# Four more source tiles of the dense products of layer 3 run beside the max-pooling layer, and early products are handed out by the load of TensorE

## The chip, the core and the metric

The kernel runs on one core of a Trainium2 chip. The time is the device time of one launch in microseconds (us). Five engines work side by side, each through its own instructions in order: TensorE (PE in the profile; PEld is its loading of weights), VectorE (DVE), ScalarE (ACT), GpSimd (POOL) and SyncE (SP). SP, ACT and POOL also issue transfers between the main memory and the buffers on the chip.

## The reference

A graph network on 6250 nodes and 100000 edges that are sorted by their target. `x` has 256 features, the hidden layers 512.

```python
def _sage_mean(h, src, dst, n, deg, W_self, W_neigh, b):
    msum = segment_sum(h[src], dst, num_segments=n)
    return h @ W_self + (msum / clip(deg, 1.0)[:, None]) @ W_neigh + b
def _sage_pool(h, src, dst, n, deg, W_pool, b_pool, W_self, W_neigh, b):
    hp = relu(h @ W_pool + b_pool)
    hmax = segment_max(hp[src], dst, num_segments=n)
    hmax = where(deg[:, None] > 0, hmax, 0.0)
    return h @ W_self + hmax @ W_neigh + b
def _sage_gcn(h, src, dst, n, deg, W_neigh, b):
    msum = segment_sum(h[src], dst, num_segments=n)
    return ((msum + h) / (deg + 1.0)[:, None]) @ W_neigh + b

h = maximum(layernorm(x), 0.0)
h = _sage_mean(h, ...)      # layer 1
h = _sage_pool(h, ...)      # layer 2, max-pooling
h = _sage_gcn(h, ...)       # layer 3
h = _sage_mean(h, ...)      # layer 4
return x + h @ W_fc + b_fc
```

## The kernel before

**Tiles.** The nodes are cut into 49 node tiles of 128 (`NT`), the edges into 782 edge tiles of 128 (`T`). For an edge tile, POOL gathers the rows of the 128 source nodes from a table in main memory by an indirect transfer, one instruction for each tile. Where a node tile has very many edges (12 node tiles in layer 1, the first 23 in layers 3 and 4, `H3` = 23) the sum is computed another way: a dense table of counts, how many edges lead from each node of a source tile to each node of the node tile, is multiplied with the rows of the source tile on TensorE. So layer 3 has 254 gathers for node tiles 23 to 48, and dense products for 23 node tiles x 49 source tiles. One dense product is a pair of matmuls, one with the high and one with the low part of the rows (L637 and L632). Its counts are loaded as 8-bit numbers (`ae` early, `ac` late) and widened by ACT (`aw`, `af`).

**Layer 2** goes through all 782 edge tiles in six blocks, in the order 100, 130, 180, 220, 100 and 52 tiles. Per edge tile (counted by `at`): POOL gathers the rows `X` (L1870), DVE takes one step of a running maximum (L1843), and SP stores the stepped rows for every two tiles (L1849). At the end of a block the maximum is carried on (`carry`): TensorE transposes the last rows (`ptcf`, L1536), DVE scans along them (L1548), TensorE turns the result back (`pcf`, L1576), and SP stores a mended row (L1582). Beside this `done2(d)` finishes the node tiles 48 to 0 one after the other: it gathers the maxima (`tot`, L1678), transposes them (L1710), multiplies with the weights (L1717, L1720, L1723), splits the result in a high and a low part (L1730 to L1739) and stores them in the table `tab_r` that layer 3 gathers from (L1746, L1747). When a node tile is begun follows the list `PACE`.

**Early products.** The result of a node tile is at once a source tile of layer 3. For source tiles 10 to 41 (`EARLY`) the dense products are taken while layer 2 still runs: four source tiles make a batch, and a batch has 23 units, one for each node tile. A unit is: SP loads its counts (`ae`, 64 KB, L1802, six units ahead, 14 buffers), ACT widens them (`aw`, L1789), ACT lays the sum so far into the accumulator (`pd<-acc`, L1782), TensorE does four pairs (L632, L637), and ACT takes the sum out (`acc<-pd`, L1774). In all these are 736 pairs. They are handed out by `early.advance(...)` after each edge tile, in an even line from `at` = 320 to 752.

**Layer 3** (`sums`) issues the 254 gathers into a ring of 10 row buffers (L549); for each one DVE makes a one-hot matrix (`hot`, L545) and TensorE multiplies the two (L571, L574). Between them a `Hub` hands out its list of other work evenly over 228 of the gathers: the products of the source tiles that were not early, in four chunks for each node tile, (0, 4), (4, 10), (42, 45) and (45, 49), 23 x 17 = 391 pairs; then `turn_to_4` (L2039), which loads rows `own` and starts the stream of counts for layer 4; then 46 products of layer 4. The counts `ac` come by ACT's queue (L1970), four chunks ahead, and each load is issued when a buffer comes free; ACT widens the chunk after the next (L1979). `done3` (L2049) finishes a node tile on DVE.

So the order of each engine's work is fixed in the program; what is free is when each one gets there.

Of the kernel before, what the change touches and what calls it, by code (L numbers as in the profile page):

```python
# [34 lines left out]
UP3 = float(2 ** 12)  # L35
ROOM3, SEEN3 = float(2 ** 28), float(2 ** 11)
EARLY = (10, 42)
MADE_AT = 64
EARLY_AT = 310
SLOTS = (10, 14)  # L40
PACE = ((112, 0), (318, 19), (612, 37), (746, 49))
# [49 lines left out]
def fast_path(  # L91
# [18 lines left out]
    FH = W1_self.shape[1]  # L110
    FO = W_fc.shape[1]
    NT = (N + P - 1) // P
# [3 lines left out]
    T = (E + P - 1) // P  # L116
# [11 lines left out]
    for d in range(NT):  # L128
        m, s = _edges_below(d * P, E, N)
        m1, s1 = _edges_below((d + 1) * P, E, N)  # L130
# [9 lines left out]
    for d in range(NT):  # L140
        m, s = _edges_below(d * P, E, N)
        m1, s1 = _edges_below((d + 1) * P, E, N)
# [7 lines left out]
    H1, H3, H4 = HUB  # L150
# [105 lines left out]
    at = 0  # L256
# [390 lines left out]
    ahead = upto2.enter_context(tc.tile_pool(name="ahead", bufs=1, side="right"))  # L647
# [805 lines left out]
    with tc.tile_pool(name="fl2c", bufs=1) as ck, ExitStack() as late:  # L1453
# [244 lines left out]
        def done2(d):  # L1698
            tots, th = totals(d)
            apart = EARLY_AT < at < T - 72  # L1700
            for _ in range(6):
                yield
            hm = tots[0]
            for t in tots[1:]:
                nc.vector.tensor_tensor(hm, hm, t, op=ALU.max)
            yield
            yield from apart_by(3 if apart else 0)
            pt = bank(pst, "pt", "pt_hTf", (KH, P))
            for j in range(KH):
                nc.tensor.transpose(pt[:, j, :], hm[:, j * P : (j + 1) * P], ident)  # L1710
            yield
            hT = wk.tile([P, KH, P], F32, name="hTf")
            nc.scalar.copy(hT, pt)  # L1713
            yield
            pm = bank(psb if EARLY_AT < at < T - 40 else psd, "pb", "pm_prf")
            for k in range(KI):
                nc.tensor.matmul(pm, th[:, k, :], usA[:, k, :], start=(k == 0), stop=False)  # L1717
            yield
            for k in range(KI):
                nc.tensor.matmul(pm, th[:, KI + k, :], usB[:, k, :], start=False, stop=False)  # L1720
            yield
            for c in range(KH):
                nc.tensor.matmul(pm, hT[:, c, :], un[:, c, :], start=False, stop=(c == KH - 1))  # L1723
                if c == 1:
                    yield
            yield
            yield
            yield
            hi, lo = r2 = row_parts(d)
            nc.scalar.copy(hi, pm)  # L1730
            yield
            yield from apart_by(2 if apart else 0)
            while d == last_begun and not last_turn:
                yield
            with behind(last_turn):
                nc.tensor.matmul(pm, minus_r, hi, start=False, stop=True, skip_group_check=True)
            yield
            yield from apart_by(2 if apart else 0)
            nc.scalar.copy(lo, pm)  # L1739
            look_at(d, hi, hT)  # L1740
            if EARLY[0] <= d < EARLY[1]:
                ready.append((d, r2))
                if len(ready) == BATCH or d == EARLY[0]:
                    early_products()
            yield from apart_by(8 if apart else 0)
            nc.sync.dma_start(tab_r[d * P : (d + 1) * P, :FH], hi.bitcast(F32))  # L1746
            nc.sync.dma_start(tab_r[d * P : (d + 1) * P, FH:], lo.bitcast(F32))  # L1747
            yield
# [9 lines left out]
                    held_by[d] = last[i]  # L1758
                last[i] = d
        assert all(d >= EARLY[0] for d in held_by.values())  # L1760
        early_all = H3 * (EARLY[1] - EARLY[0])
        ready = []
        early = Hub(look=6)
        early_pool, split_pool = [], []
# [26 lines left out]
        def early_products():  # L1791
            batch = dict(ready)
            ss = sorted(batch)
            ready.clear()
            over.update({s: len(early.work) + H3 * len(ss) for s in ss})
            for d in range(H3):
                got = {}
                loaded.append(got)

# [52 lines left out]
        def paced(at):  # L1852
            for (a0, n0), (a1, n1) in zip(PACE, PACE[1:]):
                if at < a1:
                    break
            return n0 + (n1 - n0) * (at - a0) / (a1 - a0)

        tiles, begun2, begun_at = [], 0, 0
        ends = []
        now = []  # L1860
        at = 0
        for b in reversed(range(NB)):
# [3 lines left out]
            for s0 in range(0, tb, G2):  # L1866
                X = (xmore if at // G2 % 2 else xpool).tile([P, G2, FH], F32, name="X2")
                for k in range(G2):
# [44 lines left out]
                    if copies and not hub.left():  # L1913
                        copies.pop(0)()
                    if at > EARLY_AT + 10:
                        early.advance(math.ceil(early_all * (at - EARLY_AT - 10)
                                                / (T - 40 - EARLY_AT)))
                    if b == 0 and s0 == 0 and k == 0:
                        for _ in finding:
                            pass  # L1920
# [83 lines left out]
    with ExitStack() as on:  # L2004
# [44 lines left out]
        with tc.tile_pool(name="fl3", bufs=2) as wk:  # L2049
# [36 lines left out]
                nc.sync.dma_start(xq[d * P : (d + 1) * P, :], q[:, :FO])  # L2086
                yield 1

            late = ((0, 4), (4, KEPT), (EARLY[1], 45), (45, NT))
            Z3 = {s: tuple(v[:, slot[s], :] for v in kept_rows) for s in range(KEPT)}  # L2090
            with tc.issue_after(kept_stores[-1].ins):
                for s0, s1 in ((EARLY[1], NT),):
                    Z3.update(resident(zw, tab_r, FH, s0, s1))
            block = stream(zw, [(d, s0, s1) for d in range(H3) for s0, s1 in late], zw, ahead=1)
            todo = []
            work = []
            for d in range(H3):
                work += dense([s for s0, s1 in late for s in range(s0, s1)], lambda s, d=d: block(d, s), lambda s: Z3[s], FH, psd,
                              lambda acc, d=d: todo.append(done3(d, acc)), own=d)
            work += [turn_to_4] + turns[0][1]  # L2100
            sums(wk, psg, tab_r, FH, srcE, keyE, jb, H3, done3, 10, Hub(work), wait=14, todo=todo,
# [683 lines left out]
```

## Time and profile before

| | us |
|---|---|
| median of three runs | 2477.61 |
| lowest and highest of them | 2477.28, 2480.75 |
| the profiled execution, its own time | 2482.45 |
| its span, first to last instruction | 2480.6 |
| layer 2 with early products, in the trace | 1116 to 1760 |
| layer 3, in the trace | 1784 to 2146 |

The share of the span in which each engine is busy is 86% for TensorE, 77% for DVE, 58% for ACT and 70% for POOL; the mean granted clock of TensorE is 0.939 of full speed. These are averages over stages with different limits, so the rows further down are taken from the two stages of the change. In such rows a time in brackets, or behind the second bar, is how long the engine stood idle just before, and the arrow names what ended that idle time. Issuing of transfers by SP and ACT isn't counted as busy.

### The profile page before, as it was taken

What the parts mean: (1) busy time and instruction counts of PE and PEld (TensorE: products, weight loads), DVE (VectorE), ACT (ScalarE), POOL (GpSimd) and SP (SyncE); (2) the same over time, 40 slices, a digit from 0 to 9 for tenths busy, and PEclk for the clock granted to TensorE, in tenths of its full rate; (3) what the DMA queues carried; (4) which work ended last, traced back from release to release, by engine and by line L of the source; (5) the groups of instructions that cost most, each with busy time, mean ns of one, the idle gap of its engine ahead of it and who ended that gap; (6) DMA issues with size and microseconds to landing.
All of it is one profiled execution on the core that took longest, in us unless ns stands there. A gap on an engine that the chain in (4) does not pass through costs nothing.

```text
span 2480.6 us, 35381 instructions
## 1 busy us (share of the span) xinstructions
PE 2143.6 (86%) x9402; PEld 1239.8 (50%) x9402; DVE 1915.2 (77%) x5404; ACT 1430.8 (58%) x2891; POOL 1739.2 (70%) x2013
## 2 busy tenths in 40 slices
PE   4689999999688477479979995999799998799997
PEld 2356666676444233134434442455344444477776
DVE  7899987785789898978868788786567776477655
ACT  5898878676378898855545663655222222244443
POOL 5477776677566776777767777777477777477776
PEclk9799999999899688689989997999899999999999
DMA  9677777777999999999999999999899999899997
GB/s 314 197 232 240 223 209 213 218 221 242 294 334 317 329 366 349 332 349 363 361 312 358 356 361 365 321 360 348 296 378 405 407 407 407 310 351 335 335 305 237
DMA packets 381103, 784.91 MB, mean 316 GB/s; under 512 B 59374, under 2 KB 175830, under 8 KB 380860
## 3 DMA queue, kind: packets, MB, share of 16 engines
q0 software_dynamic: 135184, 471.64, 56.6%
q1 hardware_dynamic: 178984, 252.38, 28.2%
q10 hardware_dynamic: 66724, 58.54, 7.3%
q8 instruction: 76, 1.25, 0.2%
q14 instruction: 135, 1.11, 0.1%
HBM read 573.21 MB, written 209.94 MB: 316 GB/s over the span
## 4 chain that ended last, share of the span: by engine, by line
PE 37%; DMA 35%; DVE 15%; issue 5%; POOL 4%; ACT 3%; ACTq 0%; POOLq 0%; DVEq 0%; SPq 0%
DMA X<-rows,srcIf 13%; PE pd L632 6%; PE pd L637 6%; PE pd L629 4%; DVE run L1843 4%; DMA rows<-X 3%; DMA xq<-acc 3%; DMA ring<-tab_s,srcE 3%; PE pm_w L292 3%; POOL X L1870 3%; DVE X L1843 3%; PE pm_hp L1278 3%; PE pg L571 2%; PE pg L574 2%; PE pm_hp L1272 2%
## 5 line engine op out<-in xcount | busy, mean ns | idle before, releaser
L1870 POOL DMA_INDIRECT X<-rows,srcIf x782 | 746.5, 955 | 302.5 <-issue 151.5
L1843 DVE SCALAR_TENSOR_TENSOR run<-run,samef,X 128x512 f32<-128x512 f32 x758 | 572.6, 755 | 76.5 <-DMA X<-rows,srcIf 70.7
L549 POOL DMA_INDIRECT ring<-tab_h,srcT x402 | 389.8, 970 | 174.9 <-issue 40.5
L1979 ACT CAST af<-ac 128x768 fp32r<-128x768 fp8e4 (+3 forms) x299 | 217.5, 735 | 352.9 <-PE pd L629 122.4
L549 POOL DMA_INDIRECT ring<-tab_r,srcE x254 | 258.4, 1017 | 99.1 <-issue 39.4
L1843 DVE SCALAR_TENSOR_TENSOR X<-X,samef,run 128x512 f32<-128x512 f32 x379 | 282.2, 745 | 54.7 <-DMA X<-rows,srcIf 22.8
L549 POOL DMA_INDIRECT ring<-tab_s,srcE x254 | 245.3, 966 | 94.8 <-PE pg L569 25.3
L603 DVE SCALAR_TENSOR_TENSOR acc<-pg,M,acc 128x256 f32<-128x256 f32 (+2 forms) x556 | 281.3, 532 | 31.5 <-PE pg L574 21.3
L574 PE MATMUL pg<-ring,hot 128*128 128x256 f32 (+1 forms) x656 | 293.3, 455 | 0.0
L637 PE MATMUL pd<-kept_rows,aw 128*128 128x512 f32 x552 | 277.0, 584 | 0.0
L571 PE MATMUL pg<-ring,hot 128*128 128x259 f16 (+1 forms) x656 | 212.0, 326 | 35.5 <-DMA ring<-tab_h,srcT 14.5
L632 PE MATMUL pd<-kept_rows,ae 128*128 128x512 f16 x552 | 215.0, 390 | 7.0 <-DMA ae<-tab_a 5.3
L1774 ACT COPY acc<-pd 128x512 f32<-128x512 f32 x184 | 107.8, 586 | 181.8 <-PE pd L637 181.5
L637 PE MATMUL pd<-Z1h,af 128*128 128x256 f32 x588 | 194.8, 364 | 0.4 <-ACT af L1306 0.4
L1723 PE MATMUL pm_prf<-unf,hTf 128*128 128x512 f32 x384 | 188.6, 615 | 1.1 <-ACT hTf L1713 1.1
L458 PE MATMUL pb<-hm,hs 128*128 128x196 bf16 x480 | 102.2, 271 | 92.3 <-DVE hm L442 60.2
L545 DVE TENSOR_SCALAR hot<-iota_bf,keyE 128x128 fp32r<-128x128 bf16 x508 | 137.7, 297 | 54.8 <-PE pg L574 28.1
L629 PE MATMUL pd<-zt,af 128*128 128x512 f32 x598 | 165.5, 396 | 2.4 <-ACT af L1979 2.4
L632 PEld LDWEIGHTS <-ae 128*128 128x128 fp8e4 x736 | 71.0, 96 | 186.4 <-issue 171.3
L632 PE MATMUL pd<-Z1l,A 128*128 128x259 f16 x588 | 158.5, 280 | 0.0
L574 PEld LDWEIGHTS pg<-ring,hot 128*128 128x128 f32 x656 | 130.8, 199 | 53.7 <-issue 45.2
L464 ACT ACTIVATE A<-pb 128x392 fp8e4<-128x392 f32 x240 | 116.8, 497 | 60.6 <-PE pb L458 59.7
(439 smaller groups left out, 5122.3 us busy)
## 6 DMA issues: line engine op xcount, KB each, us to landing
rows<-X SPq DMA_DIRECT2D x385, 256.0 KB
rows<-hpf SPq DMA_DIRECT2D x49, 256.0 KB
X<-rows,srcIf POOLq DMA_INDIRECT x782
th<-tab_t SPq DMA_DIRECT2D x48, 256.0 KB
ae<-tab_a SPq DMA_DIRECT2D x184, 64.0 KB
tab_a<-A ACTq DMA_DIRECT2D x15, 784.0 KB
ac<-tab_a ACTq DMA_DIRECT2D x115, 96.0 KB
tab_t<-th SPq DMA_DIRECT2D x37, 256.0 KB
```

The lines of the kernel that those rows point to most:

```text
L545: nc.vector.tensor_scalar(hot[j], iota_b, keyT[:, j - jb : j - jb + 1], None, op0=ALU.is_equal)
L549: nc.gpsimd.indirect_dma_start(out=ring[:, j % deep, :].bitcast(F32), out_offset=None, in_=table, in_offset=bass.IndirectOffsetOnAxis(ap=s ...
L571: nc.tensor.matmul(pg[:, : F + counts], hot[j].bitcast(BF16)[:, 1::2], X.bitcast(F16)[:, 2 * F : 3 * F + counts], start=(k == 0), stop=False)
L574: mm = nc.tensor.matmul(pg[:, :F], hot[j], X[:, :F], start=False, stop=(k == n - 1))
L603: nc.vector.scalar_tensor_tensor(acc[d], half, m, acc[d], op0=ALU.mult, op1=ALU.add)
L629: nc.tensor.matmul(hold[0], a[0], z, start=(s == ss[0]), stop=(s == ss[-1]))
L632: nc.tensor.matmul(hold[0][:, : F + extra], a[1], z[1][:, : F + extra], start=(s == ss[0] and hold[1]), stop=False, **more)
L637: nc.tensor.matmul(hold[0][:, :F], a[0], z[0], start=False, stop=(s == ss[-1]), **more)
L1723: nc.tensor.matmul(pm, hT[:, c, :], un[:, c, :], start=False, stop=(c == KH - 1))
L1843: stepped[:] = [nc.vector.scalar_tensor_tensor(put, held, st, row, op0=ALU.mult, op1=ALU.max)]
L1870: nc.gpsimd.indirect_dma_start(out=X[:, k, :], out_offset=None, in_=tab_p, in_offset=bass.IndirectOffsetOnAxis(ap=srcI[:, t : t + 1], axis=0),
L1979: nc.scalar.copy(wide[i][:, :n, :], got[i][:, :n, :])
```

## The change

A ninth early batch takes source tiles 6 to 9, for node tiles 0 to 11 only (`EARLY_KEPT`). It adds 12 units with 48 pairs to the early products (784 in place of 736) and takes them out of layer 3 (343 in place of 391), where the chunk (4, 10) becomes (4, 6) for these 12 node tiles. The rate at which early pairs are handed out is no longer even: `early_to` counts each node tile that is begun by `PACE` as 17 pairs (`TILE_PAIRS`) and keeps the sum of both even.

```diff
+EARLY_KEPT = (6, 12)
+TILE_PAIRS = 17
...
-            if EARLY[0] <= d < EARLY[1]:
+            if EARLY_KEPT[0] <= d < EARLY[1]:
                 ready.append((d, r2))
-                if len(ready) == BATCH or d == EARLY[0]:
+                if len(ready) == BATCH or d == EARLY_KEPT[0]:
                     early_products()
...
-        early_all = H3 * (EARLY[1] - EARLY[0])
+        early_all = H3 * (EARLY[1] - EARLY[0]) + EARLY_KEPT[1] * (EARLY[0] - EARLY_KEPT[0])
...
-            over.update({s: len(early.work) + H3 * len(ss) for s in ss})
-            for d in range(H3):
+            h = H3 if ss[0] >= EARLY[0] else EARLY_KEPT[1]
+            over.update({s: len(early.work) + h * len(ss) for s in ss})
+            for d in range(h):
...
+        def early_to(at):
+            a0, a1 = EARLY_AT + 10, T - 32
+            n0 = paced(a0)
+            load = early_all + TILE_PAIRS * (NT - n0)
+            return math.ceil(load * min(1.0, (at - a0) / (a1 - a0)) - TILE_PAIRS * (paced(min(at, PACE[-1][0])) - n0))
...
-                        early.advance(math.ceil(early_all * (at - EARLY_AT - 10)
-                                                / (T - 40 - EARLY_AT)))
+                        early.advance(early_to(at))
...
-            late = ((0, 4), (4, KEPT), (EARLY[1], 45), (45, NT))
+            late = [((0, 4), (4, EARLY_KEPT[0] if d < EARLY_KEPT[1] else KEPT), (EARLY[1], 45),
+                     (45, NT)) for d in range(H3)]
...
-            block = stream(zw, [(d, s0, s1) for d in range(H3) for s0, s1 in late], zw, ahead=1)
+            block = stream(zw, [(d, s0, s1) for d in range(H3) for s0, s1 in late[d]], zw, ahead=1)
...
-                work += dense([s for s0, s1 in late for s in range(s0, s1)], lambda s, d=d: block(d, s), lambda s: Z3[s], FH, psd,
+                work += dense([s for s0, s1 in late[d] for s in range(s0, s1)], lambda s, d=d: block(d, s), lambda s: Z3[s], FH, psd,
```

In the changed program the lines of the early products and of layer 2 stand two to nine further down (L632 is L634, L637 is L639, L1536 is L1538, L1802 is L1805, L1849 is L1852, L571 is L573).

TensorE's program around the transposes `ptcf` at the end of the block of 220 edge tiles, before; the rows L632 and L637 are early pairs, L1720 and L1723 belong to `done2`:

```order
L1720 MATMUL pm_prf_18142<-usB_10239,th2_17821 128x512 x2
L632 LDWEIGHTS ae_17989
L632 MATMUL pd_18127<-kept_rows1_11381,ae_17989 128x512
L637 MATMUL pd_18127<-kept_rows0_11380,aw_18098 128x512
L632 LDWEIGHTS ae_17989
L632 MATMUL pd_18127<-kept_rows1_11381,ae_17989 128x512
L1536 MATMUL ptcf_18380<-identf_97,X2_18359 128x128 x4
L637 MATMUL pd_18127<-kept_rows0_11380,aw_18098 128x512
L1723 MATMUL pm_prf_18142<-unf_10240,hTf_18131 128x512 x2
```

The same place after:

```order
L639 MATMUL pd_18373<-r2h_13_18102,aw_18349 128x512
L634 LDWEIGHTS ae_18235
L634 MATMUL pd_18373<-r2l_12_17893,ae_18235 128x512
L639 MATMUL pd_18373<-r2h_12_17892,aw_18349 128x512
L1712 MATMUL pt_hTf_18404<-identf_97,tot_18282 128x128
L1538 MATMUL ptcf_18658<-identf_97,X2_18640 128x128 x4
L1712 MATMUL pt_hTf_18404<-identf_97,tot_18282 128x128 x3
```

Before, these transposes follow 495 early pairs, of a batch whose rows are in `kept_rows`; after, they follow 562, of the batch with source tiles 10 to 13 (`r2h_13`, `r2l_12`).

SyncE's queue around the store of the mended row of that block (L1582, `fixf`), before; `rows2<-X2` are the stepped rows, `ae` the counts of early pairs:

```order
L1849 DMA rows2_72<-X2_18529 128x512
L1802 DMA ae_18551<-tab_a_70 128x256
L1849 DMA rows2_72<-X2_18548 128x512
L1802 DMA ae_18573<-tab_a_70 128x256
L1849 DMA rows2_72<-X2_18570 128x512
L1802 DMA ae_18597<-tab_a_70 128x256
L1582 DMA rows2_72<-fixf_18506 128x512
L1802 DMA ae_18623<-tab_a_70 128x256
```

After:

```order
L1852 DMA rows2_72<-X2_18771 128x512
L1805 DMA ae_18627<-tab_a_70 128x256
L1852 DMA rows2_72<-X2_18791 128x512
L1693 DMA th2_18969<-tab_t_67 128x512
L1852 DMA rows2_72<-X2_18813 128x512
L1805 DMA ae_18650<-tab_a_70 128x256
L1852 DMA rows2_72<-X2_18829 128x512
L1584 DMA rows2_72<-fixf_18769 128x512
L1748 DMA tab_r_68<-kept_rows0_11380 128x512
```

Behind the block's end fewer loads of counts stand between the stores of rows, and a load for `done2` and a store of a finished node tile have come in.

TensorE's program in layer 3 about the 91st gather, before; `pg` is the sum over gathered rows, `pd` a dense sum:

```order
L571 MATMUL pg_21262<-ring_20161,hot_21224 128x512
L574 MATMUL pg_21262<-ring_20161,hot_21224 128x512
L632 LDWEIGHTS ac_21168
L632 MATMUL pd_21207<-zt42_20149,ac_21168 128x512
L637 MATMUL pd_21207<-zt42_20149,af_21245 128x512
L632 LDWEIGHTS ac_21183
L632 MATMUL pd_21207<-zt42_20149,ac_21183 128x512
L637 MATMUL pd_21207<-zt42_20149,af_21286 128x512
L571 LDWEIGHTS hot_21239
```

After:

```order
L573 MATMUL pg_21447<-ring_20349,hot_21407 128x512
L576 MATMUL pg_21447<-ring_20349,hot_21407 128x512
L639 MATMUL pd_21477<-kept_rows0_11380,af_21478 128x512
L634 LDWEIGHTS ac_21393
L634 MATMUL pd_21477<-kept_rows1_11381,ac_21393 128x512
L639 MATMUL pd_21477<-kept_rows0_11380,af_21478 128x512
L573 LDWEIGHTS hot_21426
```

Where two pairs of dense products stood between two gathers, there are now fewer than two on average, and each node tile's list is in another place.

## Rows read from the trace of the kernel before

**Rows 1.** By stretches: window, length, busy PE, PEld, DVE, ACT, POOL, clock, DMA, GB/s
```profile
1116.00:1545.00 429.00, 385.49 (x1423) 187.07 (x1422) 349.98 (x558) 231.07 (x452) 316.50 (x334) 0.95 1.00 354
1545.00:1760.00 215.00, 207.71 (x763) 102.18 (x761) 165.09 (x249) 119.35 (x234) 157.11 (x165) 0.98 0.99 341
...
1845.00:2085.00 240.00, 236.09 (x1011) 106.94 (x1010) 180.28 (x409) 62.74 (x114) 184.65 (x179) 0.99 1.03 407
```

**Rows 2.** Timeline of POOL in layer 2: start, duration, instruction, [idle before <-releaser]
```profile
1399.27 0.95 POOL L1870 DMA_INDIRECT X<-rows,srcIf  x1 [0.30 <-issue]
1400.52 0.95 POOL L1870 DMA_INDIRECT X<-rows,srcIf  x1 [0.30 <-DVE X L1843]
```

**Rows 3.** POOL's groups, 1116 to 1760 us: count, busy, mean ns, idle before
```profile
L1870 POOL DMA_INDIRECT X<-rows,srcIf x463 | 441.1, 953 | 157.1 <-issue 96.0 <-DVE X L1843 20.4 <-DVE run L1843 20.1
```

**Rows 4.** POOL's groups, 1784 to 2104 us
```profile
L549 POOL DMA_INDIRECT ring<-tab_r,srcE x241 | 245.6, 1019 | 88.1 <-issue 37.5 <-PE pg L574 16.6 <-DVE oddI L79 13.9
```

**Rows 5.** Timeline of POOL in layer 3
```profile
1953.87 0.95 POOL L549 DMA_INDIRECT ring<-tab_r,srcE  x1 [0.30 <-PE pd L637]
...
1956.37 1.36 POOL L549 DMA_INDIRECT ring<-tab_r,srcE  x1 [0.30 <-issue]
...
1960.80 1.50 POOL L549 DMA_INDIRECT ring<-tab_r,srcE  x1 [0.30 <-DMA ring<-tab_r,srcE]
```

**Rows 6.** Timeline of TensorE in layer 3
```profile
1950.60 0.39 PE L571 MATMUL pg<-ring,hot 128*128 128x512 f16 x1
...
1951.06 0.39 PE L632 MATMUL pd<-kept_rows,ac 128*128 128x512 f16 x1
...
1951.52 0.39 PE L632 MATMUL pd<-kept_rows,ac 128*128 128x512 f16 x1
```

**Rows 7.** Timeline of TensorE at the end of the block of 220
```profile
1516.45 0.39 PE L632 MATMUL pd<-kept_rows,ae 128*128 128x512 f16 x1
1544.65 1.09 PE L1536 MATMUL ptcf<-identf,X 128*128 128x128 f32 x4 [27.81 <-DVE X L1843]
```

**Rows 8.** SyncE's waits, 1116 to 1790 us: line <- released by: us, times, longest
```profile
SPq L1802 <- PE pd L632: 19.0, 18, 3.6
SPq L1802 <- PE pd L637: 16.7, 22, 1.9
```

**Rows 9.** ScalarE's groups by form, 1116 to 1784 us
```profile
L1789 ACT CAST aw<-ae 128x512 fp32r<-128x512 fp8e4 x183 | 113.7, 622 | 16.4 <-DMA ae<-tab_a 16.3
L1774 ACT COPY acc<-pd 128x512 f32<-128x512 f32 x184 | 107.8, 586 | 181.8 <-PE pd L637 181.5
```

**Rows 10.** POOL's groups at the end of layer 3, 2104 to 2146 us
```profile
L549 POOL DMA_INDIRECT ring<-tab_r,srcE x13 | 12.8, 984 | 11.0 <-PE pg L574 8.5 <-issue 1.9 <-PE pd L629 0.3
```

**Rows 11.** Timeline of POOL there
```profile
2110.86 1.05 POOL L549 DMA_INDIRECT ring<-tab_r,srcE  x1 [3.01 <-PE pg L574]
...
2119.94 0.95 POOL L549 DMA_INDIRECT ring<-tab_r,srcE  x1 [3.21 <-PE pg L574]
```

**Rows 12.** Timelines of TensorE, ScalarE and SyncE there
```profile
2109.55 0.61 PE L571 MATMUL pg<-ring,hot 128*128 128x512 f16 x1 [5.34 <-DVE hot L545]
...
2107.78 0.40 ACT L332 CAST q<-acc 128x256 fp32r<-128x256 f32 x1 [13.12 <-DMA own<-tab_r]
...
2085.77 6.04 SPq L2045 DMA_DIRECT2D own<-tab_r  x5
```

**Rows 13.** Timeline of ScalarE in layer 3: loads of counts (ACTq) and their casts
```profile
1896.92 0.33 ACTq L1970 DMA_DIRECT2D ac<-tab_a  x1
...
1903.65 0.51 ACT L1979 CAST af<-ac 128x384 fp32r<-128x384 fp8e4 x1 [1.56 <-DMA ac<-tab_a]
...
1905.49 0.33 ACTq L1970 DMA_DIRECT2D ac<-tab_a  x1
...
1913.40 0.84 ACT L1979 CAST af<-ac 128x768 fp32r<-128x768 fp8e4 x1 [2.95 <-DMA ac<-tab_a]
```

**Rows 14.** All waits, 1783 to 2120 us
```profile
PE pd L637 <- ACT af L1979: 2.0, 2, 1.7
```

## The prediction

> **What bounds the kernel now.** I read the view by stretches first, then the POOL groups of the two stages that the change touches, then the timelines of POOL and TensorE inside them, and last the views of waits. The two stages are layer 2, from where the early products begin (1116 us) to its last gather (1760 us), and layer 3 (1784 to 2146 us).
>
> By stretches [rows 1], TensorE looks like the bound of both: 385.5 of 429 us and 207.7 of 215 us busy in layer 2, and 236.1 of 240 us in the middle of layer 3. POOL shows only 316.5 of 429 and 184.7 of 240 us. The reader is to distrust both numbers: between two gathers POOL has idle time that is the same every time. In layer 2 a gather is busy 0.95 us after 0.30 us idle, whether the row puts the idle to issue or to DVE [rows 2]. So 1.25 us is the least from one gather to the next. From 1116 to 1760 us there are 334 + 165 = 499 POOL operations [rows 1], nearly all of them gathers of 0.953 us [rows 3]; 499 x 1.25 = 624 of 644 us. POOL is issuing for 97% of the stretch, and all waits together cost at most 20 us. In layer 3, 241 gathers of 1.019 us [rows 4] at 0.30 us between make 241 x 1.32 = 318 of the 320 us from 1784 to 2104. The gap is 0.30 us there too, whether the releaser is a product (PE pd L637) or issue [rows 5]. Had TensorE held POOL up, these gaps would be longer than the plain ones. POOL's issue bounds both stages; TensorE has just kept step.
>
> The Trainium skill ("Perfetto Trace Analysis", Identifying the Most-Contended Engine) would have GpSimd judged by its occupancy, and says that the busy share of matmuls is a poor measure for TensorE. By the first half POOL has 23% of room in layer 3 and is not the bound, which would leave rival A; the constant gap of 0.30 us [rows 2, 5] speaks against that reading, and the trace agrees with the second half. The sum below goes by the gap.
>
> **The change part by part.** It moves 48 pairs of products (12 node tiles x 4 source tiles) from layer 3 to layer 2, with 12 loads of 64 KB. It also hands out all 784 early pairs by a new rule: 1.96 pairs per edge tile up to the 612th, then 1.48, where before it was 736/432 = 1.70 throughout. (Worked out: 784 pairs plus 17 for each of the 29.9 node tiles still to begin are 1292 over 430 edge tiles, 3.00 each; of these, tiles begun take 17 x 18/294 = 1.04 up to the 612th and 17 x 12/134 = 1.52 after.)
>
> *TensorE in layer 3.* From one product or gather's pair to the next is 0.46 us [rows 6]. The 48 pairs are 48 x 0.46 = 22 us. Before, 391 + 47 = 438 items are spread over 254 - 14 - 12 = 228 gathers, 1.92 each, so a gather costs TensorE 2.92 x 0.46 = 1.34 us; after, 390 items, 1.71 each, 2.71 x 0.46 = 1.25 us. POOL takes 1.32 us for it. TensorE goes from level with POOL to a little below it. Since POOL sees no wait beyond 0.30 us, I take 0 for this; the ends are -22 us (TensorE bound it after all) and +3 us (the work after the products now falls three gathers earlier).
>
> *TensorE in layer 2.* The 22 us come in here, and most pairs earlier. The cover is a wait: at the end of the block of 220 edge tiles TensorE comes at 1516.8 us to the transposes L1536 and stands 27.8 us until DVE's last running maximum [rows 7]. In program order 495 early pairs stand before these transposes, and 562 after the change: 67 x 0.46 = 31 us more, so TensorE comes there at about 1548, 3 us late instead of 28 us early. So the wait is filled. Behind it 736 - 495 = 241 pairs remained, now 222, 9 us less, in the stretch that was fullest (207.7 of 215 us). I take 0 for TensorE itself: the last gather is POOL's.
>
> *SyncE.* SyncE's stores of the stepped rows free the buffers that POOL gathers into. Its loads of counts stand in the same queue, and waited for products 19.0 + 16.7 = 36 us [rows 8]. A load waits where TensorE is late with the product that frees its buffer, and TensorE is latest just behind the wait of 27.8 us. With that wait filled, less is late there. Only part of it reached POOL, whose whole loss is 20 us. I take -2 us, between -10 and +7 (the second end is rival C).
>
> *ScalarE.* 12 more widenings of 0.622 us and 24 copies of 0.586 us [rows 9], 21.5 us, beside 231 us of work in 429 us [rows 1]: hidden, 0. If they had no cover they would delay products, not gathers. In layer 3, 12 casts become shorter.
>
> *Transfers.* 12 x 64 KB = 0.79 MB go from layer 3, where 407 GB/s moved at a busy share of 1.03, to layer 2 at 354 GB/s [rows 1]: -1.9 us and +2.2 us if transfers bound both stages. In layer 3 POOL's gathers take 1.019 us against 0.953 us; some are 1.2 to 1.5 us [rows 5], which fits full queues, and 241 x 0.066 = 16 us is the most that a lighter load could return. The load falls by 0.6%, so I take -1.5 us there and +1 us in layer 2.
>
> *The end of layer 3.* POOL waits 11.0 us over 13 gathers for TensorE, less 13 x 0.30 = 3.9, which is 7.1 us too much, most of it at two places [rows 10, 11]. The reason isn't TensorE's load: at 2109.55 it stood 5.3 us for the one-hot matrix from DVE. DVE was held by ScalarE, whose cast stood behind the loads of layer 4's counts and waited 13.1 us, put down to the rows own<-tab_r, whose loads SyncE began at 2085.8 us [rows 12]. The step that issues these loads comes after 343 of 390 items and not after 391 of 438, three gathers earlier; everything in its shadow moves with it. I take 0, between -7 and +3 us.
>
> Sum: 0 + 0 - 2 + 0 - 1.5 + 1 + 0 = -2.5 us. On the profiled execution, 2482.45 us with a span of 2480.6 us, that is 2480. This execution lies 4.8 us above the median of the three runs, 2477.61, so against that median I say **2475 us**, with its own range from 2469.5 to 2480.5.
>
> **The rivals.**
>
> A. *TensorE bounds layer 3.* For it: 236.1 of 240 us busy, and its 1.34 us per gather is no less than POOL's 1.32. Against it: the gap that never grows. Then 228 x (1.34 - 1.25) = 20 us and the 2.5 us above go: 2455 us.
>
> A2. *The end of layer 3 loosens.* With fewer products TensorE has caught up before the two waits [rows 11], and the ring of ten gathered rows absorbs them: -7.1 - 2.5 gives 2468 us. Against it: the releaser behind the first is a transfer's landing [rows 12].
>
> B. *Slower: the look-ahead of layer 3's counts becomes too short.* The loads run four chunks ahead, each when a buffer comes free, and a cast comes 6.7 and 7.9 us after its load [rows 13]; the cast waits for the landing. Four chunks were 17 products, 17/1.92 x 1.33 = 11.8 us. For the 12 node tiles they are 13, 13/1.71 x 1.33 = 10.1 us. The cast itself takes 0.5 to 0.8 us [rows 13], so some 0.9 us must be left: from a delay of 9.2 us on TensorE waits, and POOL behind it through the ring. At 10.5 us that is 12 x 1.3 = 16 us, less what the ring holds, say 5: +11, 2489 us. Against it: 7.9 is below 9.2, and that stage had only 2.0 us of products waiting for a cast [rows 14].
>
> C. *Slower: layer 2's queue fills.* TensorE comes to the block's end with 31 us more of work in front of it and, without the wait, has no idle time left to catch up with. Loads of counts then find their 14 buffers in use earlier and SyncE's waits double, another 36 us. POOL lost at most 20 us beside the first 36; at a fifth this is +7, 2485 us. It decides if TensorE comes to L1536 later than some 1560 us, 15 us after DVE is done.
>
> D. *It does nothing*: the gains are taken up by other waits, 2477 us.
>
> **How the numbers follow.** About 0.2% (5 us) is what a measurement of this kernel can tell from no change. Forecast 0.50, of which 0.14 is faster by more than 5 us and 0.36 within; A 0.16 and A2 0.11, faster; D 0.06, same; B 0.08 and C 0.09, slower. Faster 0.14 + 0.16 + 0.11 = 0.41, same 0.36 + 0.06 = 0.42, slower 0.17. Both signs outside the forecast have weight, so the range takes in A2 and C whole, and leaves out most of A (0.14) and of B (0.06): 2460 to 2486.
>
> **What the profile after would show.** Right: the wait before L1538 (L1536 before) of the block of 220 falls from 27.8 us to under 4; SyncE's waits for products fall well below 36 us; layer 3's gathers still start 1.32 us apart with TensorE's busy share there down by about 7 points; layer 3 has the same length within 3 us. Wrong: if layer 3 from its first to its last gather is over 10 us shorter, TensorE bound it (A); if products there wait for casts over 10 us, B; if SyncE's waits for products grow and POOL's gaps with them, C. The forecast falls if either stage changes its length by more than 8 us.

## The result

The changed kernel is a little slower: 2487.72 us (median of 20 runs) against 2481.45 us (20 runs of the kernel before beside them), a ratio of 1.0028 (95% interval 1.0017 to 1.0039). In a second comparison it was 1.0020 (1.0005 to 1.0035). The forecast was 2475 us in a range to 2486. A part of the miss is the base: the median of three runs that it went out from, 2477.61, is 3.8 us below that of twenty. The rest of the miss, 8.9 us, is the gain of 2.5 us that didn't come and a cost of 6.3 us in its place.

The profiled execution after took 2496.45 us, at the upper end of its runs, so a single difference between the two profiles says little; below, stages are compared over several profiles. By stretches of the changed kernel (columns as in [rows 1]; the first three windows answer to the three there):

```profile
1118.00:1547.00 429.00, 407.15 (x1510) 197.20 (x1509) 344.70 (x548) 249.85 (x485) 309.56 (x328) 0.97 1.00 347
1556.00:1771.00 215.00, 203.16 (x739) 98.95 (x738) 164.93 (x249) 114.01 (x223) 154.47 (x163) 0.97 0.98 343
1856.00:2096.00 240.00, 224.80 (x931) 104.08 (x930) 177.20 (x403) 60.65 (x115) 174.91 (x176) 0.99 1.02 398
```

TensorE's busy time moved as the working said: 407 us where it had 385, 203 where it had 208, and 225 of 240 us in layer 3 where it had 236. POOL issued 328 operations in 429 us where it had issued 334, and 176 in 240 us where it had issued 179. So TensorE's load was moved as planned, and the engine that sets the pace became slower in both stages.

TensorE at the end of the block of 220 edge tiles, after:

```profile
1556.49 0.60 PE L1538 MATMUL ptcf<-identf,X 128*128 128x128 f32 x4
1568.18 0.66 PE L1578 MATMUL pcf<-identf,cTf 128*128 128x128 f32 x2 [9.85 <-DVE cTf L1554]
```

The wait of 27.8 us [rows 7] is gone: the row L1538 has no bracket. A wait of 9.85 us for DVE's scan comes in behind it. SyncE's waits for products fell from 36 to 27 us [rows 8]:

```profile
SPq L1805 <- PE pd L639: 16.6, 22, 1.7
SPq L1805 <- PE pd L634: 10.2, 15, 2.4
```

But POOL's group of layer 2 (1119 to 1770 us) has longer idle times put down to DVE (32.7 and 18.4 us, where there were 20.1 and 20.4 [rows 3]); busy time, mean ns and idle time stand behind the bars:

```profile
L1879 POOL DMA_INDIRECT X<-rows,srcIf x461 | 437.2, 948 | 170.7 <-issue 95.0 <-DVE run L1846 32.7 <-DVE X L1846 18.4
```

At the end of layer 3 (timeline of POOL, after), the two waits of [rows 11] are still there, the first one earlier and longer, and the wait for layer 4's first gather, 17.66 us before, is 13.38 us:

```profile
2121.59 0.95 POOL L551 DMA_INDIRECT ring<-tab_r,srcE  x1 [6.42 <-PE pg L576]
...
2138.19 1.20 POOL L551 DMA_INDIRECT ring<-tab_r,srcE  x1 [3.26 <-PE pg L576]
2159.05 0.96 POOL L551 DMA_INDIRECT ring<-tab_s,srcE  x1 [13.38 <-DMA ac<-tab_a]
```

### The profile page after: what moved, and what is told of

Read it like the earlier page. It is cut to its first block, busy times and chain, and to the rows that moved or that the text cites. A ratio compares the mean times of both kernels' runs of the same rounds, so it can differ in the third digit from the quotient of the medians.

```text
span 2494.7 us, 35434 instructions
## 1 busy us (share of the span) xinstructions
PE 2163.9 (87%) x9402; PEld 1253.8 (50%) x9402; DVE 1915.7 (77%) x5404; ACT 1444.8 (58%) x2927; POOL 1726.1 (69%) x2013
## 4 chain that ended last, share of the span: by engine, by line
PE 40%; DMA 32%; DVE 16%; issue 5%; ACT 4%; POOL 3%; SPq 0%; ACTq 0%; DVEq 0%; POOLq 0%
DMA X<-rows,srcIf 12%; PE pd L639 6%; PE pd L634 6%; PE pd L631 5%; DMA xq<-acc 5%; DVE run L1846 4%; DMA rows<-X 3%; PE pm_hp L1280 3%; PE pm_w L294 3%; DVE X L1846 3%; POOL X L1879 2%; PE pm_hp L1274 2%; PE pg L573 2%; DMA ring<-tab_s,srcE 2%; PE pg L576 2%
## 5 line engine op out<-in xcount | busy, mean ns | idle before, releaser
L1987 ACT CAST af<-ac 128x640 fp32r<-128x640 fp8e4 (+4 forms) x299 | 211.3, 717 | 353.8 <-PE pd L631 125.6
L551 POOL DMA_INDIRECT ring<-tab_r,srcE x254 | 251.2, 989 | 113.9 <-PE pg L576 37.2
L639 PE MATMUL pd<-kept_rows,aw 128*128 128x512 f32 x600 | 300.4, 585 | 0.0
L634 PE MATMUL pd<-kept_rows,ae 128*128 128x512 f16 x600 | 235.0, 392 | 12.3 <-ACT pd L1784 6.7
L573 PE MATMUL pg<-ring,hot 128*128 128x259 f16 (+1 forms) x656 | 211.5, 325 | 37.3 <-DMA ring<-tab_r,srcE 22.6
L1776 ACT COPY acc<-pd 128x512 f32<-128x512 f32 x196 | 115.0, 586 | 203.0 <-PE pd L639 202.7
L639 PE MATMUL pd<-Z1h,af 128*128 128x256 f32 x588 | 194.8, 364 | 1.0 <-ACT af L1308 1.0
L634 PEld LDWEIGHTS <-ae 128*128 128x128 fp8e4 x784 | 75.9, 97 | 201.2 <-issue 187.5
L634 PE MATMUL pd<-Z1l,A 128*128 128x259 f16 x588 | 158.5, 280 | 0.0
```

Of the source, the lines that this page charges most:

```text
L551: nc.gpsimd.indirect_dma_start(out=ring[:, j % deep, :].bitcast(F32), out_offset=None, in_=table, in_offset=bass.IndirectOffsetOnAxis(ap=s ...
L573: nc.tensor.matmul(pg[:, : F + counts], hot[j].bitcast(BF16)[:, 1::2], X.bitcast(F16)[:, 2 * F : 3 * F + counts], start=(k == 0), stop=False)
L634: nc.tensor.matmul(hold[0][:, : F + extra], a[1], z[1][:, : F + extra], start=(s == ss[0] and hold[1]), stop=False, **more)
L639: nc.tensor.matmul(hold[0][:, :F], a[0], z[0], start=False, stop=(s == ss[-1]), **more)
L1987: nc.scalar.copy(wide[i][:, :n, :], got[i][:, :n, :])
```

## The experiments

The runs fell on two kinds of chip. On the one, the kernel before takes 2480 us, as in the first measurement. On the other it takes 2944 to 2948 us: an instruction of POOL or DVE lasts as long there, but POOL waits far longer in layer 2 (figures below). Verdicts on the change are taken from the first kind only.

Stage lengths, read from the starts of POOL's gathers in each profile, are used throughout. Layer 2 is from the 311th to the last of its gathers, layer 3 from its first gather to the first of layer 4, so its passage to layer 4 is in it. Three profiles with the old program of layer 2 (before, f4, k3) lie within 1.7 us there, four with the changed one (changed twice, k1, k2) within 8.0 us. A wait of POOL is its idle time beyond the constant gap, 0.305 us to three places.

| kernel, first kind of chip | ratio to before (95%) | layer 2 | layer 3 |
|---|---|---|---|
| before | 1 | 654.7 | 361.3 |
| changed, first and second comparison | 1.0028, 1.0020 | 664.5, 660.3 | 363.8, 361.9 |
| f1: the rule alone | 0.9997 (0.9980 to 1.0015) | 658.6 | 359.0 |
| f2: the ninth batch alone | 1.0074 (1.0052 to 1.0097) | 669.4 | 363.0 |
| f4: short list in layer 3 alone | 0.9997 (0.9985 to 1.0010) | 653.0 | 359.8 |
| k1: changed, counts six chunks ahead | 1.0021 (1.0008 to 1.0035) | 656.5 | 362.4 |
| k2: changed, six buffers for sums | 1.0010 (0.9994 to 1.0027) | 657.6 | 358.0 |
| k3: before, 138 pairs less in layer 3 | 1.0047 (1.0034 to 1.0059) | 653.4 | 371.7 |
| k4: f2 with 36 of the 48 pairs left out | 1.0057 (1.0039 to 1.0074) | 665.5 | 361.1 |

**The parts of the change.** The theories were S2 (layer 2 pays for the denser early part), S3 (layer 3 pays for its shorter lists) and, later, S4 (the rule gains, the batch costs). The changed kernel itself stood beside the parts:

> The changed kernel itself, on the chip of the three runs beside it, as their measure: +4 to +10 us by every theory if this chip is like that of the first measurement, where before is near 2480 us.

1.0020, or +5 us. The rule alone keeps the batch out:

```diff
-EARLY_KEPT = (6, 12)
+EARLY_KEPT = (10, 0)
```

> Only the new rule of handing out. On the chip with times near 2946 us this was 10 us faster (interval 2 to 18). S2 (layer 2 pays for the denser early part): +5 to +9 us. S3 (layer 3 pays): within 2 us. Third theory, S4, that the rule helps by filling TensorE's wait of 28 us and the ninth batch costs: -8 to -2 us.

No change, -1 us (-5 to +4): S2 in its first form falls, and so does the first half of S4, as the rule alone isn't a gain either. The batch alone goes back to the even line:

```diff
-                        early.advance(early_to(at))
+                        early.advance(math.ceil(early_all * (at - EARLY_AT - 10)
+                                                / (T - 40 - EARLY_AT)))
```

> Only the ninth batch, in an even line. S2: 0 to +3 us. S3: +5 to +9 us. S4: +8 us or more, since the rule's gain is missing.

+18 us, as S4 had forecast, though not for its reason (a missing gain of the rule). Most of the loss is in one place: POOL's waits behind the 730th gather of layer 2 are 20.1 us, 3.7 before. DVE at the end of the block of 100 edge tiles, ninth batch alone (timeline: start, duration, instruction, idle time before):

```profile
1711.49 0.73 DVE L1550 TENSOR_TENSOR_SCAN segf<-keepTf,ptcf 128x128 f32<-128x128 bf16 x2 [16.19 <-PE ptcf L1538]
...
1728.91 0.69 DVE L1581 TENSOR_TENSOR fixf<-fixf,pcf 128x512 f32<-128x512 f32 x1 [6.37 <-PE pcf L1578]
```

POOL there:

```profile
1711.72 0.94 POOL L1879 DMA_INDIRECT X<-rows,srcIf  x1 [5.60 <-PE ptcf L1538]
...
1718.63 0.94 POOL L1879 DMA_INDIRECT X<-rows,srcIf  x1 [4.72 <-DVE run L1846]
```

DVE comes to the scan and stands 16.2 us until TensorE has made the transposes. DVE works in order, so the running maximum behind the scan stands too, and POOL finds no free buffer. In the kernel before, the same scan had no wait:

```profile
1703.28 0.42 DVE L1548 TENSOR_TENSOR_SCAN segf<-keepTf,ptcf 128x128 f32<-128x128 bf16 x1
```

The programs explain it. Between the transposes of the block of 220 and these there stand 690 - 495 = 195 early pairs before, 735 - 520 = 215 with the batch in an even line, 736 - 562 = 174 in the changed kernel. TensorE in this stretch before, with the batch alone, and in the changed kernel (second profile; columns as in [rows 1]):

```profile
1544.70:1694.70 150.00, 147.24 (x555) 72.16 (x556) 114.84 (x168) 92.32 (x180) 110.81 (x117) 0.98 0.99 343
1541.10:1710.80 169.70, 161.47 (x608) 78.67 (x609) 121.46 (x179) 98.88 (x193) 123.26 (x130) 0.97 0.99 347
1551.80:1703.70 151.90, 140.16 (x521) 67.75 (x520) 115.61 (x170) 86.67 (x168) 110.98 (x117) 0.96 0.99 346
```

Before, TensorE is nearly always busy and makes the transposes some 8 us ahead of DVE's scan. The even line puts 14 us more of work in front of them: 9 us are the 20 pairs, and most of the rest is eight products of `done2`, which now stand in front too. TensorE's only long wait in the stretch, for DVE's scan of the block of 220, grows from 2.8 to 8.2 us as well. So it comes 20 us later after the transposes of the block of 220, and DVE stands. The new rule takes 41 pairs out of the stretch again, and with them about two thirds of the batch's cost (18 against 5 to 7 us).

Layer 3 alone has the old layer 2 and the short list:

```diff
-            late = ((0, 4), (4, KEPT), (EARLY[1], 45), (45, NT))
+            late = [((0, 4), (4, 6 if d < 12 else KEPT), (EARLY[1], 45), (45, NT)) for d in range(H3)]
```

> Layer 2 as before, layer 3 with the short list (48 pairs left out of the sums of 12 node tiles). S2 and S4: -3 to +1 us, since the cost lies in layer 2. S3: +5 to +9 us, with POOL's waits in the middle of layer 3 at 8 us or more, behind DVE's waits for the stores of xq.

No change, -1 us (-4 to +2): the 22 us less of TensorE's work are worth nothing in layer 3. But a part of S3's picture is there: DVE waits for a buffer until the store of a node tile's result (`xq`) from it has landed in main memory. These waits in its layer 3, 1778 to 2098 us:

```profile
DVE acc L603 <- DMA xq<-acc: 45.7, 13, 13.0
DVE acc L2063 <- DMA xq<-acc: 19.5, 9, 3.5
```

Before, from 1784 to 2104 us, it was 36 us:

```profile
DVE acc L601 <- DMA xq<-acc: 26.2, 12, 3.6
DVE acc L2054 <- DMA xq<-acc: 9.9, 4, 5.1
```

These longer waits of DVE cost nothing here: POOL's waits from the 60th to the 127th gather of layer 3 are 0.3 us, where S3 had 8 us or more.

**The same parts on the other kind of chip.** There they gave 0.9966 (0.9940 to 0.9993) for the rule, a gain of 10 us that the first kind doesn't show, 1.0009 (0.9982 to 1.0037) for the batch, 1.0019 (0.9998 to 1.0041) for the changed layer 2 with the old list in layer 3, and 0.9989 (0.9960 to 1.0018) for the short list. POOL waits 170 to 200 us in layer 2 there, where it waits 19 to 36 us on the first kind. Behind the 730th gather they are 20 to 29 us there with the old program of layer 2 (e4, and h3, m1 and m2 below), where they are 4 us here. So the place that costs the batch 18 us is late there in any case; that this hides the batch's cost is likely, but not shown.

> Only the new rule of handing out (with 736 early pairs, 1.88 per edge tile up to the 612th, then 1.40); no ninth batch, layer 3 as before. Theory S2, that layer 2 pays for the denser early part (loads of counts and stores of rows crowd the transfers, and the gathers' rows land late for DVE): +5 to +9 us against the kernel before, and POOL's waits from 1118 to 1776 us some 10 us above the 20 us of before. Theory S3, that layer 3 pays for its shorter lists: within 2 us of before.

> Only the ninth batch: 784 early pairs in an even line of 1.81 per edge tile, and 343 pairs left in layer 3. S2: 0 to +3 us, since the line is only 6% denser, and TensorE's wait before the transposes of the block of 220 stays at 15 us or more. S3: +5 to +9 us, with DVE in layer 3 waiting over 50 us for the stores of xq (36 us before).

> Layer 2 as in the changed kernel (784 early pairs, new rule), but layer 3 keeps its old list of 391 pairs, so that 48 pairs are added twice to the sums of 12 node tiles. S2: +7 us or a little more. S3: within 2 us of before.

> Layer 2 as before (736 early pairs in the old line), but layer 3 has the short list of 343 pairs, so that 48 pairs are left out of the sums of 12 node tiles. S2: -3 to 0 us. S3: +5 to +9 us. If TensorE's work bounded layer 3 in spite of POOL's even gaps: -15 us or more.

**Is it TensorE's time that the batch costs?** Only the first of the four pairs of each unit is kept, in the even line:

```diff
+                part = ss if ss[0] >= EARLY[0] else ss[:1]
-                work = dense(ss, rows_at, lambda s: batch[s], FH, psd,
+                work = dense(part, rows_at, lambda s: batch[s], FH, psd,
...
+                work += [lambda: None] * (len(ss) - len(part))
```

> The ninth batch in the even line with all loads, casts and copies but one of four pairs in each of its 12 units (36 pairs left out, 16.6 us of TensorE), same chip. TensorE's time is what the batch costs in layer 2: 0 to +6 us against before, POOL's 20 us of waits at the end of the block of 100 gone. Its loads and ScalarE's work cost: +14 us or more, as with all four pairs (+18 us).

+14 us, on the boundary of the second answer, but the trace shows why this isn't one for loads and casts: DVE stands at the same scan for TensorE,

```profile
1720.92 0.73 DVE L1550 TENSOR_TENSOR_SCAN segf<-keepTf,ptcf 128x128 f32<-128x128 bf16 x2 [14.59 <-PE ptcf L1538]
```

and in this program, too, 735 pairs stand before these transposes. The ninth batch's pairs come last, so the ones that I left out stood behind the place. What stands before it are pairs of the older batches that the even line brings forward to make room. The experiment was badly aimed. POOL's waits behind the 730th gather are 14.0 us, 10 more than before, and layer 2 is 12 us longer than with the old program; so most of the cost comes from where other pairs come to stand, and not from the batch's own pairs. What its loads and casts cost isn't told.

**Does TensorE bound layer 3 after all?** A far larger piece of work is taken away:

```diff
-            late = ((0, 4), (4, KEPT), (EARLY[1], 45), (45, NT))
+            late = ((0, 4), (EARLY[1], 45), (45, NT))
```

> The kernel before without the products of source tiles 4 to 9 in layer 3 (138 of 391 pairs and the own rows of node tiles 4 to 9 left out), 64 us less of TensorE's work, same chip. POOL's issue bounds layer 3: -6 to +6 us, and layer 3 with its passage to layer 4 at 355 to 366 us (361.3 before). TensorE bounds it in part: -20 us or more.

64 us less of work, and 12 us *more* time (8 to 15), most of it in layer 3 (371.7 us). No theory had that. The waits of TensorE and DVE in this layer 3, 1782 to 2120 us:

```profile
PE pd L632 <- DVE acc L2054: 36.9, 15, 5.4
...
DVE acc L2054 <- DMA xq<-acc: 23.7, 12, 4.7
DVE acc L601 <- DMA xq<-acc: 14.2, 5, 4.9
```

The first of these rows before, 1784 to 2104 us:

```profile
PE pd L632 <- DVE acc L2054: 0.6, 1, 0.6
```

A dense sum of a node tile that is done waits in TensorE's accumulator for DVE, and TensorE stands. A part of this is that DVE itself waits for a buffer for the finished sum, which is free when the store of `xq` has landed; the buffers are four, and the sums over gathers share them. It is the smaller part: DVE's waits for `xq` are 38 us, hardly more than the 36 us of before, and within the 42 us in which TensorE stands for L2054 (with L629), DVE's timeline has 10.5 us of them. For most of the rest DVE is busy with other work of its queue.

And TensorE's clock fell. One such place, in TensorE's timeline and then as a stretch by itself, 1864.6 to 1869.6 us, where the granted clock (the third figure from the end) is 0.53, almost all of it at the lower of its two levels, 1.2 GHz:

```profile
1864.59 0.58 PE L632 MATMUL pd<-kept_rows,ac 128*128 128x512 f16 x1 [5.43 <-DVE acc L2054]
1866.28 0.65 PE L632 MATMUL pd<-kept_rows,ac 128*128 128x512 f16 x1
...
1870.00 0.39 PE L632 MATMUL pd<-zt,ac 128*128 128x512 f16 x1
```

```profile
1864.60:1869.60 5.00, 5.00 (x14) 2.28 (x13) 4.04 (x10) 0.40 (x1) 1.60 (x2) 0.53 0.97 362
```

After TensorE has stood for 5.43 us a product takes 0.65 us in place of 0.39, and two of POOL's gathers come after 2.25 and 1.24 us of idle time. Over the whole of layer 3 the granted clock is 0.89 in this run, where it was 0.97 before:

```profile
1785.50:2157.20 371.70, 296.83 (x1121) 146.59 (x1120) 247.78 (x564) 72.73 (x138) 252.59 (x255) 0.89 0.99 371
1783.90:2145.20 361.30, 337.08 (x1405) 161.28 (x1405) 245.80 (x562) 91.30 (x160) 258.38 (x255) 0.97 1.00 388
```

So TensorE stands more often for DVE, and runs slower behind such stands; POOL's waits between the first and the last gather are 29 us, 8 before. No run here parts the stands from the clock, and why shorter lists bring the stands isn't shown.

**Which wait is the stall near the 100th gather?** In the second profile of the changed kernel TensorE stands there for counts and a cast, as rival B would have it:

```profile
1922.97 0.39 PE L634 MATMUL pd<-zt,ac 128*128 128x512 f16 x1 [1.51 <-DMA ac<-tab_a]
1926.58 0.79 PE L639 MATMUL pd<-zt,af 128*128 128x512 f32 x1 [2.77 <-ACT af L1987]
```

Behind the second row the granted clock is 0.51, from 1926.2 to 1929.6 us. And POOL:

```profile
1929.40 0.94 POOL L551 DMA_INDIRECT ring<-tab_r,srcE  x1 [1.95 <-PE pg L576]
...
1937.62 0.94 POOL L551 DMA_INDIRECT ring<-tab_r,srcE  x1 [2.01 <-PE pd L639]
```

Two edits on the changed kernel, the first one `deep=6` in the stream of counts, the second one six buffers:

```diff
-                    q = wk.tile([P, FH], F32, name="acc", bufs=4)
+                    q = wk.tile([P, FH], F32, name="acc", bufs=6)
...
-                 rest=12, open_accs=4, spare_hots=2)
+                 rest=12, open_accs=6, spare_hots=2)
```

> The changed kernel with counts of layer 3 loaded six chunks ahead, on a chip where before takes near 2480 us, if it can be had: the look-ahead theory (rival B): POOL waits from the 60th to the 127th gather of layer 3 under 2 us (3.6 to 9.0 us in the profiles with short list and ninth batch) and 3 to 6 us less than the changed kernel, so 0 to +3 us against before. The xq theory: waits there as before and +4 to +7 us against before.

> The changed kernel with six buffers for the finished sums of layer 3, same chip. The xq theory: POOL waits there under 2 us, 0 to +3 us against before. The look-ahead theory: +4 to +7 us.

With counts further ahead the time is 1.0021, and POOL's waits from the 60th to the 127th gather are 7.1 us, no smaller than without the edit. Its waits from 1780 to 2110 us show casts that seldom wait for a transfer (16.1 us, where they did 103.4 in the changed kernel), and yet TensorE waits for them:

```profile
ACT z L334 <- DVE acc L2063: 67.7, 20, 6.7
...
ACT af L1987 <- DMA ac<-tab_a: 16.1, 4, 9.1
PE pd L639 <- ACT af L1987: 8.2, 3, 4.0
...
DVE acc L603 <- DMA xq<-acc: 37.2, 10, 10.8
DVE acc L2062 <- DMA xq<-acc: 19.9, 7, 5.6
```

So the look-ahead isn't the cause: ScalarE has DVE's late sums (`z`) in front of the casts in its queue, and waits 67.7 us for them. With six buffers this is 14.3 us, DVE's waits for `xq` are gone from the list, and TensorE's products L639 wait for no cast any more. But POOL's waits from the 60th to the 127th gather are still 2.7 us, where the xq theory had under 2 and the changed kernel's second profile has 3.6. The short list alone (f4), with 65 us of waits for `xq`, has 0.3 us. So the buffers aren't shown to be the cause either. On this kind of chip the stall is there in the profiles with both the short list and the ninth batch, and not with the list alone; why is open. Layer 3 is 358.0 us with six buffers, the shortest of all, by 1 us. The time, 1.0010, lies between; it can be told neither from before nor, surely, from the changed kernel.

On the other kind of chip the four k runs were 1.0067 (1.0031 to 1.0103) for the counts six chunks ahead, 1.0046 (1.0010 to 1.0082) for six buffers, 1.0034 (1.0001 to 1.0067) without the 138 pairs and 1.0020 (0.9980 to 1.0059) for the quarter of the batch. The changed kernel itself wasn't run there, so the first two have no measure. Taking away 64 us of TensorE's work gains nothing there either.

> The changed kernel with the counts of layer 3 loaded six chunks ahead in place of four. If the stall near the 100th gather of layer 3 (3.6, 7.6 and 9.0 us of POOL waits in the profiles with the short list and the ninth batch, where TensorE waits for loads and casts of counts) is rival B's short look-ahead: those waits fall under 2 us and the time by 3 to 6 us. If they come from DVE's waits for the stores of xq: unchanged within 2 us.

> The changed kernel with six buffers in place of four for the sums of layer 3 that DVE finishes and whose store of xq it waits for. If the stall near the 100th gather comes from there: POOL waits under 2 us there and 3 to 6 us less time. If it is the look-ahead of counts: unchanged within 2 us.

> The kernel before without the products of source tiles 4 to 9 in layer 3 (138 of 391 pairs and the own rows of node tiles 4 to 9 left out): 64 us less of TensorE's work there. POOL's issue bounds layer 3: within -6 and +6 us. TensorE bounds it in part (its busy share was 98%): -20 us or more.

> The ninth batch in the even line (18 us slower than before), with all its loads, casts and copies, but only the first of four pairs in each of its 12 units (36 pairs left out): 16.6 us less of TensorE's work in layer 2, the rest unchanged. If TensorE's time is what the batch costs there: +1 to +6 us against before. If its loads and ScalarE's work are: +14 us or more.

**Buffers alone, and the price of loads.** The last two runs are edits of the kernel before: the six buffers, and every fourth load of early counts issued twice.

```diff
+                    if i % 4 == 0:
+                        again = early_pool[0].tile([P, BATCH, P], F8, name="ax", bufs=2)
+                        nc.sync.dma_start(again.bitcast(BF16), tab_a[d, :, ss[0] : ss[-1] + 1, :])
```

> The kernel before with six buffers in place of four for the finished sums of layer 3. With its long lists DVE waited 36 us for the stores of xq, but POOL only 7 us, at the end. If buffers are worth something by themselves there: -2 to -5 us. If they only mend what the short lists bring: within 2 us of before.

> The kernel before with every fourth load of early counts issued a second time into a buffer that nobody reads: 46 loads, 3.0 MB more in layer 2. By the rate of that stretch (354 GB/s) that is +8.5 us if transfers are its limit; 0 if they have room. If loads delay the gathers by more than their own time, as a cost of 6 us for 0.79 MB in the changed kernel would say: +20 us or more.

Both fell on the other kind of chip: 1.0013 (0.9985 to 1.0040) and 0.9998 (0.9969 to 1.0028), on 2944 us. The buffers are no gain that shows, and 3.0 MB more of loads cost between -9 and +8 us there, so +20 us is excluded for that chip. For the first kind both stay open.

## Why the prediction was wrong

**Right: POOL's issue bounds layer 3, and TensorE's 22 us are worth nothing there.** The short list alone gave -1 us, and 64 us less gave no gain either, though it lengthened the layer by other waits. Reading POOL's constant gap of 0.30 us, and not the busy shares, was what told this; rival A, which had the busy share of 98% on its side, falls. The Trainium skill's measure for GpSimd ("Perfetto Trace Analysis", Identifying the Most-Contended Engine), its occupancy, shows 77% there; the runs decide for the gap.

**Right: TensorE's wait at the end of the block of 220 is filled.** I had TensorE there 31 us later, at 1548 us. It came at 1556.5 us in a trace whose gathers were 8 us late by then (the 631st at 1548 us in place of 1540 us). In the four profiles with this program it came 6 to 8 us behind that gather; my working said 8.

**Wrong: "I take 0 for TensorE itself" and "-2 us" for SyncE in layer 2.** This is the step that failed. With +1 us for transfers these terms were -1 us. Measured, layer 2 with the changed program is 664.5, 660.3, 656.5 and 657.6 us long, 659.7 in the mean, and with the old one 654.7, 653.0 and 653.4, 653.7 in the mean: +6 us. What grew is the one thing that I had held to be at most 20 us and about to shrink, POOL's waits: 25.1 us in the mean of the four, 18.9 us in the three, which is the whole difference. SyncE's waits for products did fall by 9 us as I had thought, but POOL's didn't fall with them. What POOL waits for is DVE, and DVE waits 81 us in the mean of these four profiles for gathered rows to land (72 to 88), against 74 us in the three (70 to 77). That is spread over many places; POOL's longest single wait is 4.4 us in the profile shown above. 3.7 of the 6 us lie ahead of the 631st gather, where the early pairs are denser than before. The profile of the rule alone has 658.6 us, 24.2 us of POOL's waits and 79 us of DVE's too, in a program whose time didn't change. So the runs don't settle whether the 0.79 MB more, the denser loads, or the order in which stores come brings it: the cause stays open. I had priced the transfers by their bytes alone.

**Not seen: what the rule is worth.** I named the stretch behind the block of 220 as the fullest and counted 9 us less of pairs in it, but priced that at 0, since the last gather is POOL's. This stretch decides whether DVE meets TensorE at the next block's transposes: with 20 pairs more there, and not less, the batch costs 18 us. Rival C had a lag of TensorE in mind, at the transposes of the block before, and its price through SyncE; the way that the even line showed goes through DVE, which stands at the scan. That C's 2485 us is near the measured time is luck: SyncE's waits were to double, and fell.

**Layer 3's own terms.** I took -1.5 us for transfers. The three changed profiles have 363.8, 361.9 and 362.4 us, against 361.3, 359.0 and 359.8 us without the batch: +2.7 us in the mean, hardly more than profiles of one program differ by. The last of the three without the batch has the short list, so the list alone isn't what costs it. The gathers did become shorter (251 to 255 us in all, 258 before), but POOL's waits between them grew by 8 to 14 us in these three profiles. The end of layer 3 moved forward with its shadow, as I said: 7 to 8 us less from the last twelve gathers to layer 4's first one, and 7 to 10 us more of waits in the sixty gathers ahead of them, so rival A2 falls too. (The 11.0 us that I gave to TensorE there are all of POOL's idle time; [rows 10] put 8.8 us of it down to TensorE.) The stall near the 100th gather is in rival B's place, but the look-ahead isn't its cause; what is stays open. I had the waits for the stores of `xq` in the view of all waits and left them out, since nothing waited for DVE then.

**The sum**: +6 and +2.7 make 8.7 us by the profiles, where the medians have 5.3 and 6.3 us. Profiles of one run each don't add up closer than that. Even from the base of twenty runs the sign of the sum would have been wrong.

## What to carry to other kernels

Moving work off a busy engine pays only if that engine holds up the one that sets the pace. Look at the gaps of the pace-setter: if they don't grow where the busy engine is late, there is nothing to win. Where work is moved *to*, count what comes to stand between the last wait of the receiving engine and the next hand-over that others need; here 14 us more in such a place cost 18 us, while 22 us less elsewhere gained nothing. And less work for an engine can mean that it stands more often for the others: with 64 us less TensorE stood 42 us for DVE, and its clock fell behind such stands.

## What was not expected of the hardware

Taking 64 us of TensorE's work out of a stage of 361 us made it 10 us longer (371.7 us), at a granted clock of 0.89 in this stage, against 0.97 before. TensorE had stood 5.43 us in one place there, and its products took 0.65 us in place of 0.39 for the next 5 us. And the same kernel takes 2480 us on one chip and 2946 us on another, with the same 755 ns for a step of the running maximum and 0.95 us for a gather's issue, while a profile there (of the rule alone) moves 268 GB/s over the span in place of 316 GB/s.
